# Start of a convolution and GRU kernel: loads on the software queue, taps in two parts, biases first

## The chip, the cores and the metric

The kernel runs on one core of a Trainium2 chip. Its time is the device time of one execution in microseconds. Three runs of the kernel before took 1042.65, 1043.94 and 1044.66 us; the median is 1043.94 us. One further execution was recorded with the hardware profiler; it took 1043.13 us, and the part that the profile shows, its span, is 1041.2 us. All times in this document that have the form of a place (such as "at 32.22") are us from the start of that span.

A core has a tensor engine (TensorE, in the profile PE for the products and PEld for the loads of the stationary operand), a vector engine (DVE), a scalar engine (ACT), GpSimd (POOL) and a sync engine (SP). SP, ACT and POOL can issue transfers from memory. SP and ACT issue on queues whose descriptors hardware makes (q1 and q10 in the profile); POOL issues on a software queue (q0).

## The reference

x is 16 sequences of 256 steps of 512 channels; cond is 16 x 512. The same cond serves twice: as the 16 taps of a causal depthwise convolution over time, and as the first hidden state of a GRU.

```python
    x = x + _L0_cond_ref(x, cond_2048[:, None, :])      # causal, 16 taps, one weight per tap and channel
    x = x + _L1_cond_ref(cond_2048, x, W_ih, W_hh, b_ih, b_hh)

        def cell(h, x):
            gi = x @ W_ih + b_ih
            gh = h @ W_hh + b_hh
            i_r, i_z, i_n = jnp.split(gi, 3, axis=-1)
            h_r, h_z, h_n = jnp.split(gh, 3, axis=-1)
            r = jax.nn.sigmoid(i_r + h_r)
            z = jax.nn.sigmoid(i_z + h_z)
            n = jnp.tanh(i_n + r * h_n)
            h_new = (1.0 - z) * n + z * h
            return (h_new, h_new)
```

All arithmetic is in float32. W_ih and W_hh are 512 x 1536, that is 3 MB each.

## The kernel before, in words

**Layout.** The 512 channels lie as four quarters q of 128 partitions (`NQ` = 4). Time is cut into 16 chunks of 16 steps (`CHUNKS`), a chunk's 16 steps x 16 sequences being 256 columns. For each chunk c: x is loaded into `x_nat` by eight transfers of 64 KB (`load_x`, two halves s of the steps times four quarters j); VectorE transposes it in two pieces into `xT` (`turn_units`), in front of which ScalarE copies the 15 earlier steps (`halo`); then the convolution is added up in `x1T`: a first term (x times 1 + the last tap, `first_terms`, ScalarE) and 15 taps a quarter (`tap_units`, VectorE, one instruction a tap and quarter, k = 0 of all four quarters first).

**Chunk 0** is different, since everything waits for it. Its quarters 0 and 1 are made on VectorE, with the taps of short reach first (`needed` = 14 instructions reach into the chunk's first eight steps), and its quarters 2 and 3 (`Q_PE`) on TensorE (`conv_on_tensor`): ScalarE scales an identity matrix by each tap's weights into 32 diagonal matrices `diag`, and TensorE multiplies x by them, tap after tap into one accumulator a quarter. Tap k reaches back `K - 1 - k` steps and writes the columns from `lag(k)` = 16 (15 - k) on; so columns 0 to 127 (the first eight steps) are done after the taps k = 15 to 8.

**Products.** `ni_units` makes the candidate's input products for a block of eight steps (`NI`), quarter by quarter, with W_ih's third part `wih_n`; ScalarE evicts each quarter and adds the bias `bnT` (`evict`). `pair_units` adds the input products of r and z for two steps into the accumulators `prz`, on top of the biases that `seed_rz` and `seed_nh` copied there from `b_rows`. `b_rows` comes from `spread_biases`: four products spread the bias rows `b_two` over the partitions into the accumulator `spare`, and ScalarE copies them out.

**Step** t (`step`): TensorE multiplies h by W_hh's parts R, N and Z (`recurrent`, L420), then does products of the next pair and of the next block (`other_products`); ScalarE takes r; VectorE, after its share of taps (`bulk_work`), multiplies r by N's product (`rn`, L446), transposes, adds, and ends with three scans (L472) whose result is the next h. The first `rn` on VectorE stands behind all taps that the program put in front.

**What sets the order.** The program's order is written by hand: each engine and queue works off its instructions in the order in which they are written. VectorE's taps and transpositions for the chunks 1 to 15 are units in a `Plan` with a cost and a step by which they are due; `bulk.run(0, HEAD)` does units of `HEAD` us in front of step 0, and each step does as many as the rate towards the due times asks for, five taps at most unless one is due. First terms and evictions are handed out from two lists (`firsts`, `evictions`) at the places where the program says so.

**Loads in front.** The taps' weights cond go out on SP and ScalarE; x's chunk 0 half on SP and ScalarE, half on POOL (L144); chunk 1 half on SP, half on POOL (L157); then the biases (L158 to L164) and W_ih by four transfers a part (`load_weights`: quarters 0 and 1 on SP, 2 and 3 on POOL). W_hh's twelve transfers are written later, behind `seed_nh` (L576): quarter 0 on SP, 1 on ScalarE, 2 and 3 on POOL, with R's on POOL kept behind the last part of W_ih. Before any product TensorE runs 108 tiny ones (`idle_products(PAD)`) and a drain.

Of the kernel before, what the change touches and what calls it, by code (L numbers as in the profile page):

```python
# [24 lines left out]
F32 = mybir.dt.float32  # L25
# [5 lines left out]
P = 128  # L31
L = 32
GT = 8
R, Z, N = 0, 1, 2
CHUNKS = (16,) * 16
PAD = 108
HEAD = 11.0
SYNC = mybir.DependencyInfo(mybir.DependencyClass.Sync, mybir.DependencyReason.DATA)
Q_PE = (2, 3)
NI = 8  # L40
# [35 lines left out]
def conv_gru_kernel(  # L76
# [31 lines left out]
    ps = ctx.enter_context(tc.tile_pool(name="ps", bufs=1, space=PSUM))  # L108
    ps_ni = ctx.enter_context(tc.tile_pool(name="ps_ni", bufs=2, space=PSUM))
# [9 lines left out]
    def load_x(c, queues=((nc.sync,), (nc.sync,)), behind=None):  # L119

        n = CHUNKS[c]
        t = xin.tile([P, max(CHUNKS) // 2, P], F32, tag="x_nat", name=f"x_nat_{c}")
        for s in range(2):
            for j in range(NQ):
                made = queues[s][j % len(queues[s])].dma_start(  # L125
                    out=t[32 * j + B * s : 32 * j + B * s + B, 0 : n // 2],
                    in_=x[:, starts[c] + s : starts[c] + n : 2, j * P : (j + 1) * P],
                )
                if s == j == 0 and behind is not None:
                    tc.add_manual_dep(made.ins, behind.ins.name, SYNC, reason="later in time")  # L130
        x_nat[c] = t
# [8 lines left out]
    for j in range(NQ):  # L140
        (nc.sync, nc.scalar)[j % 2].dma_start(
            out=cond_nat[32 * j : 32 * j + B, :], in_=cond[:, j * P : (j + 1) * P]
        )
    load_x(0, ((nc.sync, nc.scalar), (nc.gpsimd,)))  # L144
    nc.scalar.activation(warm, warm, AF.Sigmoid)
    ident = const.tile([P, P], F32)
    make_identity(nc, ident)
# [6 lines left out]
    bn_nat = const.tile([P, P], F32)  # L154
    nc.vector.memset(bn_nat, 0.0)

    load_x(1, ((nc.sync,), (nc.gpsimd,)))  # L157
    nc.sync.dma_start(out=b_two[0:1, :], in_=b_hh.rearrange("(o c) -> o c", o=1))  # L158
    nc.sync.dma_start(
        out=b_two[1:2, 0 : 2 * C], in_=b_ih[0 : 2 * C].rearrange("(o c) -> o c", o=1)  # L160
    )
    nc.gpsimd.dma_start(
        out=bn_nat[0:P:L, :], in_=b_ih[2 * C : 3 * C].rearrange("(j c) -> j c", j=NQ)
    )  # L164

# [1 line left out]
    wih_rz = const.tile([P, NQ, 2 * C], F32)  # L167
    wih_n = const.tile([P, NQ, C], F32)
    whh = [const.tile([P, NQ, C], F32, name=f"whh_{g}") for g in range(3)]

    def load_weights(w_sb, w, g, queues):
        return [
            queues[j].dma_start(
                out=w_sb[L * j : L * j + L],
                in_=w[j * P : (j + 1) * P, g * C : g * C + w_sb.shape[2]].rearrange(
                    "(q l) c -> l q c", l=L
                ),
            )
            for j in (0, 2, 1, 3)
        ]  # L180


    for tile_of, g in ((wih_n, N), (wih_rz, R)):
        of_wih = load_weights(tile_of, w_ih, g, (nc.sync, nc.sync, nc.gpsimd, nc.gpsimd))
    zero_z = [const.tile([P, NQ * B * 2], F32, name=f"zero_z_{i}") for i in range(2)]
    for t in zero_z:
        nc.gpsimd.memset(t, 0.0)
# [11 lines left out]
    b_rows = const.tile([P, 3, P], F32)  # L199


    xT, x1T, ni = {}, {}, {}
# [3 lines left out]
    evictions = []  # L206
# [7 lines left out]
    def turn_units(c):  # L214

        def halo():
            xT[c] = xtp.tile([P, NQ, HALO + CMAX], F32, tag="xT", name=f"xT_{c}")
            if c:
                m = CHUNKS[c - 1] * B
                nc.scalar.copy(xT[c][:, :, 0:HALO], xT[c - 1][:, :, m : m + HALO])  # L220

        def turn(a):
            o = HALO + a * PAIR
            nc.vector.transpose(  # L224
                xT[c][:, :, o : o + GT * B].rearrange("p q (a r) -> p a q r", r=L),
                x_nat[c][:, a : a + GP].rearrange("p a (q l) -> p a q l", q=NQ),
            )
            if 2 * (a + GP) == CHUNKS[c] and 4 < c + 3 < NCH:
                load_x(c + 3)

        return [(0.0, halo)] + [
            (0.7, lambda a=a: turn(a)) for a in range(0, CHUNKS[c] // 2, GP)
        ]

    def first_terms(c):

        x1T[c] = x1p.tile([P, NQ, CMAX], F32, tag="x1T", name=f"x1T_{c}")
        n = CHUNKS[c] * B

        def first(q):  # L240
            nc.scalar.activation(  # L241
                x1T[c][:, q, 0:n],
                xT[c][:, q, HALO : HALO + n],
                AF.Copy,
                scale=last1[:, q : q + 1],
            )
# [33 lines left out]
    def conv_on_tensor():  # L280

        n = CHUNKS[0] * B
        diag = const.tile([P, len(Q_PE), K, P], F32)

        def weight(k, q):
            return condT[:, q, k : k + 1] if k < K - 1 else last1[:, q : q + 1]

        for i, q in enumerate(Q_PE):
            for k in reversed(range(K)):
                nc.scalar.activation(diag[:, i, k], ident, AF.Copy, scale=weight(k, q))  # L290
        for i, q in enumerate(Q_PE):
            acc = ps_ni.tile([P, CHUNKS[0] * B], F32, tag="pni", name=f"conv_{q}")
            for k in reversed(range(K)):
                nc.tensor.matmul(  # L294
                    acc[:, lag(k) : n],
                    lhsT=diag[:, i, k],
                    rhs=xT[0][:, q, HALO : k * B + n],
                    start=(k == K - 1),
                    stop=(k == 0),
                    skip_group_check=True,  # L300
                )
            evictions.append(lambda q=q, acc=acc: nc.scalar.copy(x1T[0][:, q, 0:n], acc[:, 0:n]))


    blocks = [(t0, NI) for t0 in range(0, T, NI)]
# [39 lines left out]
    rz = [ps.tile([P, 2, P], F32, name=f"prz_{i}") for i in range(2)]  # L345
    nh = [ps.tile([P, P], F32, name=f"pnh_{i}") for i in range(2)]
    spare = ps.tile([P, 3, P], F32, name="spare")

    def mark():

        for i in range(2):
            nc.tensor.matmul(rz[i], lhsT=blank[:, 0:P], rhs=blank, start=True, stop=True)
            nc.tensor.matmul(nh[i], lhsT=blank[:, 0:P], rhs=blank[:, 0:P], start=True, stop=True)

    def idle_products(n):

        for _ in range(n):
            nc.tensor.matmul(
                spare[0:L, 0, 0:1], lhsT=blank[:, 0:L], rhs=blank[:, 0:1], start=True, stop=True
            )  # L360

    def spread_biases():
        for j in range(NQ):
            nc.tensor.matmul(
                spare[L * j : L * j + L],
                lhsT=ones,
                rhs=b_two.rearrange("o (g j c) -> o j g c", g=3, j=NQ)[:, j],
                start=True,
                stop=True,
            )  # L370
# [166 lines left out]
    bulk = Plan()  # L537
    mark()
    idle_products(PAD)
    nc.tensor.drain()  # L540
    (_, halo), *turns = turn_units(0)
    halo()
    for t in hist:
# [6 lines left out]
    for q in range(NQ):  # L550
        if q not in Q_PE:
# [2 lines left out]
                xT[0][:, q, HALO : HALO + CHUNKS[0] * B],  # L554
                last1[:, q : q + 1],
            )
    conv_on_tensor()

    taps = [fn for i, (_, fn) in reversed(list(enumerate(tap_units(0)))) if i % NQ not in Q_PE]
    needed = (NI - 1) * (NQ - len(Q_PE))  # L560
# [5 lines left out]
    for fn in taps[needed:]:  # L566
        fn()
    evictions.pop(0)()
    first_terms(1)
    give_firsts()  # L570
    evictions.pop(0)()
    spread_biases()
    nc.scalar.copy(b_rows, spare)
    seed_rz(0)
    seed_nh(0)
    for g in (R, N, Z):  # L576

        made = load_weights(whh[g], w_hh, g, (nc.sync, nc.scalar, nc.gpsimd, nc.gpsimd))
        if g == R:
            tc.add_manual_dep(made[2].ins, of_wih[0].ins.name, SYNC, reason="behind W_ih in time")  # L580
    for fn in ni_units(*blocks[0]):
        while evictions:
            evictions.pop(0)()
        fn()
    while evictions:
        evictions.pop(0)()
    for fn in pair_units(0):
        fn()
    for c in range(1, NCH):
        due = starts[c] - NI  # L590
        taps = tap_units(c)

        ahead = []
        if c + 1 < NCH:
            ahead = turn_units(c + 1) + [(0.0, lambda c=c: first_terms(c + 1))]
        at = len(taps) - AHEAD
        for cost, fn in taps[:at] + (ahead if c > 1 else []) + taps[at:]:
# [9 lines left out]
    for t in range(T):  # L607
        p, s = divmod(t, 2)
# [65 lines left out]
```

## Time and profile before

| what | value |
|---|---|
| median of three runs | 1043.94 us |
| the profiled execution, its own time | 1043.13 us |
| its span | 1041.2 us |
| TensorE products busy | 1023.8 us (98%) |
| VectorE busy | 926.6 us (89%) |
| ScalarE busy | 380.2 us (37%) |
| the chain that ended last | 96% TensorE, 1% VectorE, 1% transfers |
| first transposition of x | 7.64 |
| first product of step 0 | 32.22 |
| first `rn` of step 0 | 35.72 |
| first product of step 1 | 37.60 |

The lines of the profile are read like this. A line of the timeline or of the chain has its start and its length in us, the engine (with a q where only its sequencer or queue works), the line of the program, the operation, what it writes and reads by the program's names, the shape and a count; in square brackets stands how long the engine was idle before it and what ended that. A line of the stretches has for each engine its busy us and in brackets the number of instructions, then the clock that TensorE was granted (1.00 is full), the share of the 16 transfer engines' time, and GB/s. A line of the transfers has the size of one and the median us from issue to landing. A group by form has busy us and the mean ns of one instruction behind the bar.

### The profile page before, as it was taken

How to read it: one execution, taken by the hardware profiler on the slowest of the kernel's cores; microseconds unless marked ns; L12 is line 12 of the kernel's file. 1: busy time of each engine (PE TensorE's matmuls, PEld its weight loads, DVE VectorE, ACT ScalarE, POOL GpSimd, SP SyncE). 2: the span in 40 equal slices, each digit the busy share in tenths (PEclk: the TensorE clock that was granted, in tenths of full speed). 3: DMA queues.
4: the chain of work that ended last, by engine and by line, in shares of the span. 5: the costliest groups of instructions: out<-in, count | busy, mean ns of one | idle time of the engine just before them, and what ended most of it. 6: DMA issues, size and time to landing. Idle time of an engine off the chain costs nothing.

```text
span 1041.2 us, 71853 instructions
## 1 busy us (share of the span) xinstructions
PE 1023.8 (98%) x32952; PEld 929.9 (89%) x32952; DVE 926.6 (89%) x3606; ACT 380.2 (37%) x1520; POOL 11.4 (1%) x27
## 2 busy tenths in 40 slices
PE   7899999999999999999999999999999999999997
PEld 7789999999999999999999999999999999999986
DVE  7899999999999999999999999999999999996555
ACT  6243433434333343433334333343333334333332
POOL 4000000000000000000000000000000000000000
PEclk9999999999999999999999999999999999999999
DMA  9320100101010010100100010010000000000000
GB/s 232 93 60 8 32 14 20 30 15 27 13 34 15 15 34 6 34 14 15 35 15 25 15 33 16 14 33 7 14 15 14 14 13 5 15 15 14 14 11 17
DMA packets 40978, 27.72 MB, mean 27 GB/s; under 512 B 6686, under 2 KB 38498, under 8 KB 40676
## 3 DMA queue, kind: packets, MB, share of 16 engines
q1 hardware_dynamic: 38612, 18.52, 7.9%
q8 instruction: 257, 4.21, 1.8%
q0 software_dynamic: 1216, 3.67, 1.3%
q10 hardware_dynamic: 848, 0.95, 0.4%
q14 instruction: 45, 0.37, 0.1%
HBM read 14.73 MB, written 8.39 MB: 22 GB/s over the span
## 4 chain that ended last, share of the span: by engine, by line
PE 96%; DVE 1%; DMA 1%; ACT 0%; issue 0%; POOL 0%; SPq 0%; DVEq 0%; POOLq 0%
PE prz L420 42%; PE pnh L420 21%; PE prz L385 20%; PE pni L322 10%; PE conv L294 1%; DMA whh<-in_L_cond_W_hh_dram 1%; DMA x_nat<-in_x_dram 0%; DVE rnT L448 0%; DVE rn L446 0%; DVE zp L459 0%; DVE n L450 0%; DVE xT L224 0%; ACT zero_z L463 0%; POOL x_nat L125 0%; DVE hist L472 0%
## 5 line engine op out<-in xcount | busy, mean ns | idle before, releaser
L420 PE MATMUL prz<-whh,hist 128*32 128x128 f32 x16320 | 539.4, 273 | 2.2 <-DVE hist L472 1.3
L420 PEld LDWEIGHTS prz<-whh,hist 128*32 128x32 f32 x16320 | 449.7, 104 | 7.3 <-DVE hist L472 5.3
L267 DVE SCALAR_TENSOR_TENSOR x1T<-xT,condT,x1T 128x256 f32<-128x256 f32 (+2 forms) x930 | 377.3, 462 | 0.6 <-ACT x1T L241 0.6
L420 PE MATMUL pnh<-whh,hist 128*32 128x128 f32 x8160 | 269.6, 273 | 0.0
L385 PE MATMUL prz<-wih_rz,x1T 128*32 128x256 f32 x4096 | 268.0, 379 | 0.0
L420 PEld LDWEIGHTS pnh<-whh,hist 128*32 128x32 f32 x8160 | 226.5, 104 | 0.0
L457 ACT ACTIVATE dn<-n 128x64 f32<-128x64 f32 x256 | 67.9, 265 | 325.1 <-DVE n L450 325.1
L385 PEld LDWEIGHTS prz<-wih_rz,x1T 128*32 128x32 f32 x4096 | 128.4, 110 | 43.8
L322 PEld LDWEIGHTS pni<-x1T,wih_n 128*32 128x32 f32 x4096 | 122.4, 110 | 43.7 <-ACT ni L334 0.8
L437 ACT ACTIVATE r<-prz 128x128 f32<-128x128 f32 x256 | 70.9, 277 | 240.5 <-PE prz L420 237.7
L322 PE MATMUL pni<-x1T,wih_n 128*32 128x128 f32 x4096 | 157.9, 273 | 0.6 <-ACT ni L334 0.6
L472 DVE TENSOR_TENSOR_SCAN hist<-zero_z,dn 128x32 f32<-128x32 f32 (+1 forms) x768 | 128.5, 216 | 0.0
L446 DVE TENSOR_TENSOR rn<-r,pnh 128x128 f32<-128x128 f32 x256 | 72.3, 282 | 38.7 <-PE pnh L420 37.4
L463 ACT ACTIVATE zero_z<-zp 128x32 f32<-128x32 f32 x512 | 90.8, 226 | 6.9
L448 DVE STREAM_TRANSPOSE rnT<-rn 128x128 f32<-128x128 f32 x256 | 79.7, 311 | 8.8
L459 DVE STREAM_TRANSPOSE zp<-prz 128x128 f32<-128x128 f32 x256 | 80.8, 316 | 0.1
L334 ACT ACTIVATE ni<-pni,bnT 128x128 f32<-128x128 f32 x128 | 46.9, 367 | 75.7 <-PE pni L322 75.7
L465 DVE TENSOR_TENSOR dn<-hist,dn 128x64 f32<-128x64 f32 x255 | 58.3, 229 | 11.4
L450 DVE TENSOR_TENSOR n<-rnT,ni 128x64 f32<-128x64 f32 x256 | 57.6, 225 | 8.9
L400 DVE COPY glance<-r 1x1 f32<-1x1 f32 x256 | 34.1, 133 | 28.3 <-ACT r L437 28.2
L373 ACT COPY prz<-b_rows 128x256 f32<-128x256 f32 x128 | 48.6, 379 | 0.0
L400 DVE COPY glance<-zero_z 1x1 f32<-1x1 f32 x256 | 36.4, 142 | 7.9
(51 smaller groups left out, 214.6 us busy)
## 6 DMA issues: line engine op xcount, KB each, us to landing
out_dram<-o SPq DMA_DIRECT2D x248, 32.0 KB, 1.7
x_nat<-in_x_dram SPq DMA_DIRECT2D x118, 64.0 KB, 3.0
whh<-in_L_cond_W_hh_dram POOLq DMA_DIRECT2D x6, 256.0 KB, 14.2
wih_rz<-in_L_cond_W_ih_dram POOLq DMA_DIRECT2D x2, 512.0 KB, 10.9
wih_rz<-in_L_cond_W_ih_dram SPq DMA_DIRECT2D x2, 512.0 KB, 12.7
whh<-in_L_cond_W_hh_dram SPq DMA_DIRECT2D x3, 256.0 KB, 15.4
whh<-in_L_cond_W_hh_dram ACTq DMA_DIRECT2D x3, 256.0 KB, 9.8
x_nat<-in_x_dram POOLq DMA_DIRECT2D x8, 64.0 KB, 4.9
```

The costliest lines, as they stand in the source:

```text
L267: nc.vector.scalar_tensor_tensor(out=x1T[c][:, q, to], in0=xT[c][:, q, k * B + to.start : k * B + n], scalar=condT[:, q, k : k + 1], in1=x ...
L322: nc.tensor.matmul(hold[q][32 * j : 32 * j + 32, 0:n], lhsT=wih_n[:, kc, j * P + q * L : j * P + q * L + L], rhs=x1T[c][:, kc, o : o + n], ...
L385: nc.tensor.matmul(rz[p % 2][32 * j : 32 * j + 32], lhsT=x1T[c][:, kc, o : o + PAIR], rhs=w_rz[:, :, j * P : (j + 1) * P], start=False, st ...
L400: nc.vector.tensor_copy(glances[i][0:1], of_scalar[0:1, 0:1])
L420: product = nc.tensor.matmul(dst[32 * j : 32 * j + m], lhsT=h[0](kc), rhs=whh[g][:, kc, j * P : (j + 1) * P], start=False, stop=(kc == NQ ...
L437: of_r = nc.scalar.activation(r, pr, AF.Sigmoid)
L446: nc.vector.tensor_mul(rn, r, pnh)
L448: nc.vector.transpose(rnT, by_part(rn))
L457: nc.scalar.activation(dn_v[:, :, :, 1], n, AF.Tanh)
L459: nc.vector.transpose(zp, by_part(pz))
L463: nc.scalar.activation(z_v[:, qs, :, 1], zp[:, qs, half], AF.Sigmoid) for qs in halves
L472: nc.vector.tensor_tensor_scan(hist_g[:, lo + at : lo + end], z[:, to], dn[:, to], 0.0, op0=ALU.mult, op1=ALU.add,)
```

## The change

- x's chunks 0 and 1 are loaded by POOL alone, 16 transfers. The bias row `bn_nat` goes to SP.
- All of W_hh is issued together with W_ih: SP has quarter 0 of all parts and quarter 1 of W_ih and of R; POOL has the rest; ScalarE issues none. The dependency that held R back is gone. POOL's two clears of `zero_z` now stand behind all its transfers.
- `spread_biases` and the copy into `b_rows` stand first on TensorE and ScalarE, in front of the diagonals; a second drain stands in front of them.
- `conv_on_tensor` makes its taps in two parts. The taps k = 15 to 8 of both quarters come first, and ScalarE evicts the first eight steps' columns; the taps k = 7 to 0 come behind the candidate's first block and in front of the first input products of r and z. The accumulators are now a tile of their own and `spare`.
- Chunk 1's first terms come one by one behind the evictions of the candidate's first block. Before, all four came before that block.
- `HEAD` is 9.3 instead of 11.0, which makes 23 taps instead of 27 in front of step 0. Chunk 2's transpositions and first terms are due with chunk 1's taps, in front of the last ten of them; before they were due four steps later.

```diff
-HEAD = 11.0
+HEAD = 9.3
...
-    load_x(0, ((nc.sync, nc.scalar), (nc.gpsimd,)))
+    load_x(0, ((nc.gpsimd,), (nc.gpsimd,)))
...
-    load_x(1, ((nc.sync,), (nc.gpsimd,)))
+    load_x(1, ((nc.gpsimd,), (nc.gpsimd,)))
...
-    nc.gpsimd.dma_start(
+    nc.sync.dma_start(
         out=bn_nat[0:P:L, :], in_=b_ih[2 * C : 3 * C].rearrange("(j c) -> j c", j=NQ)
     )
...
-    for tile_of, g in ((wih_n, N), (wih_rz, R)):
-        of_wih = load_weights(tile_of, w_ih, g, (nc.sync, nc.sync, nc.gpsimd, nc.gpsimd))
+    for tile_of, w, g in (
+        (wih_n, w_ih, N),
+        (wih_rz, w_ih, R),
+        (whh[R], w_hh, R),
+        (whh[N], w_hh, N),
+        (whh[Z], w_hh, Z),
+    ):
+        second = nc.gpsimd if tile_of is whh[N] or tile_of is whh[Z] else nc.sync
+        load_weights(tile_of, w, g, (nc.sync, second, nc.gpsimd, nc.gpsimd))
...
-        for i, q in enumerate(Q_PE):
-            acc = ps_ni.tile([P, CHUNKS[0] * B], F32, tag="pni", name=f"conv_{q}")
-            for k in reversed(range(K)):
...
-            evictions.append(lambda q=q, acc=acc: nc.scalar.copy(x1T[0][:, q, 0:n], acc[:, 0:n]))
+        def taps(ks, to):
+            for i, q in enumerate(Q_PE):
+                for k in ks:
+                    nc.tensor.matmul(
+                        conv[i][:, lag(k) : n],
+                        lhsT=diag[:, i, k],
+                        rhs=xT[0][:, q, HALO : k * B + n],
+                        start=(k == K - 1),
+                        stop=(k == 0),
+                        skip_group_check=True,
+                    )
+                evictions.append(
+                    lambda i=i, q=q: nc.scalar.copy(x1T[0][:, q, to], conv[i][:, to])
+                )
+
+        return [
+            lambda: taps(range(K - 1, K - 1 - NI, -1), slice(0, NI * B)),
+            lambda: taps(range(K - 1 - NI, -1, -1), slice(NI * B, n)),
+        ]
...
+    conv = [
+        ps.tile([P, CHUNKS[0] * B], F32, name="conv_0"),
+        spare.rearrange("p g c -> p (g c)")[:, 0 : CHUNKS[0] * B],
+    ]
...
     nc.tensor.drain()
+    nc.tensor.drain()
...
-    conv_on_tensor()
+    spread_biases()
+    nc.scalar.copy(b_rows, spare)
+    needed_first, needed_later = conv_on_tensor()
+    needed_first()
...
     evictions.pop(0)()
-    first_terms(1)
-    give_firsts()
     evictions.pop(0)()
-    spread_biases()
-    nc.scalar.copy(b_rows, spare)
     seed_rz(0)
     seed_nh(0)
-    for g in (R, N, Z):
-
-        made = load_weights(whh[g], w_hh, g, (nc.sync, nc.scalar, nc.gpsimd, nc.gpsimd))
-        if g == R:
-            tc.add_manual_dep(made[2].ins, of_wih[0].ins.name, SYNC, reason="behind W_ih in time")
+    first_terms(1)
     for fn in ni_units(*blocks[0]):
         while evictions:
             evictions.pop(0)()
+            give_firsts(1)
         fn()
+    while evictions:
+        evictions.pop(0)()
+    give_firsts()
+    needed_later()
...
-        for cost, fn in taps[:at] + (ahead if c > 1 else []) + taps[at:]:
+        for cost, fn in taps[:at] + ahead + taps[at:]:
             bulk.add(cost, due, fn)
-        if c == 1:
-            for cost, fn in ahead:
-                bulk.add(cost, due + GT // 2, fn)
```

More of the change, by code (lines that the diff above doesn't have):

```diff
@@ L171, in load_weights @@
     def load_weights(w_sb, w, g, queues):
-        return [
+        for j in (0, 2, 1, 3):
             queues[j].dma_start(
@@ L178, in load_weights @@
             )
-            for j in (0, 2, 1, 3)
-        ]
-    for tile_of, g in ((wih_n, N), (wih_rz, R)):
-        of_wih = load_weights(tile_of, w_ih, g, (nc.sync, nc.sync, nc.gpsimd, nc.gpsimd))
+    for tile_of, w, g in (
[7 more added lines that the diff above has]
+        load_weights(tile_of, w, g, (nc.sync, second, nc.gpsimd, nc.gpsimd))
     zero_z = [const.tile([P, NQ * B * 2], F32, name=f"zero_z_{i}") for i in range(2)]
@@ L290, in conv_on_tensor @@
                 nc.scalar.activation(diag[:, i, k], ident, AF.Copy, scale=weight(k, q))
-        for i, q in enumerate(Q_PE):
-            acc = ps_ni.tile([P, CHUNKS[0] * B], F32, tag="pni", name=f"conv_{q}")
-            for k in reversed(range(K)):
[L294 to L300, printed above, removed]
-                )
-            evictions.append(lambda q=q, acc=acc: nc.scalar.copy(x1T[0][:, q, 0:n], acc[:, 0:n]))
+        def taps(ks, to):
[11 more added lines that the diff above has]
+                    lambda i=i, q=q: nc.scalar.copy(x1T[0][:, q, to], conv[i][:, to])
+                )
+        return [
+            lambda: taps(range(K - 1, K - 1 - NI, -1), slice(0, NI * B)),
+            lambda: taps(range(K - 1 - NI, -1, -1), slice(NI * B, n)),
+        ]
     blocks = [(t0, NI) for t0 in range(0, T, NI)]
```

## The prediction

> **What bounds the kernel now.** I read the page first (engines, slices), then the chain of waits over the first 60 us, then the timeline, the stretches and the forms of single instructions there. TensorE is busy 98% of the span, and past the first steps each step takes 3.92 us (rn starts at 91.16 and 95.08), an order of products that the change leaves alone. So the change is worth what it does before step 0's end and in the dozen steps behind it. The chain of waits there:
>
> ```profile
> 2.98 4.39 DMA x_nat<-in_x_dram
> ...
> 7.64 1.32 DVE xT L224 x2
> ...
> 9.09 11.82 PE conv L294 x64
> 20.91 0.82 PE spare L364 x8
> ...
> 21.76 0.49 ACT b_rows L573
> ...
> 22.33 9.64 DMA whh<-in_L_cond_W_hh_dram
> 31.97 0.25 issue
> 32.22 2.00 PE prz L420 x29
> ```
>
> Read it downwards: x lands, its transposition, all 32 taps of the convolution, the biases, and only then, from ScalarE's queue behind its copies, the last quarter of W_hh, which lands 9.6 us later. Then the stretches (busy us of PE, PEld, DVE, ACT, POOL; granted clock; DMA share; GB/s):
>
> ```profile
> 26.00:28.00 2.00, 1.82 (x36) 0.82 (x28) 2.00 (x6) 0.37 (x1) 0.00 (x0) 1.00 1.05 309
> 28.00:30.00 2.00, 0.00 (x0) 0.00 (x0) 2.00 (x7) 0.00 (x0) 0.00 (x0) 1.00 1.06 247
> 30.00:32.00 2.00, 0.00 (x0) 0.00 (x0) 1.65 (x5) 0.00 (x0) 0.00 (x0) 0.91 0.67 131
> 32.00:34.00 2.00, 1.78 (x31) 1.60 (x35) 0.00 (x0) 0.00 (x0) 0.00 (x0) 0.50 0.07 20
> ```
>
> TensorE idles over 4 us, and its first step then runs at a granted clock of 0.50. The DMA engines are full until 30 us: bytes bound this part almost as much as the late issue. VectorE is busy nearly as long, with taps put ahead of step 0:
>
> ```profile
> 29.59 2.05 DVE L267 SCALAR_TENSOR_TENSOR x1T<-xT,condT,x1T 128x256 f32<-128x256 f32 x5
> ...
> 34.84 0.14 DVE L400 COPY glance<-r 1x1 f32<-1x1 f32 x1 [3.20 <-ACT r L437]
> 35.72 0.29 DVE L446 TENSOR_TENSOR rn<-r,pnh 128x128 f32<-128x128 f32 x1 [0.73 <-PE pnh L420]
> ```
>
> Its taps end at 31.64 and step 0's rn starts at 35.72: at most 4 us can be had before VectorE itself is the bound. This rn is my yardstick; the next step's first product follows 1.88 us later (37.60).
>
> **The loads.** x goes through GpSimd's queue alone. Four issues there take 2.21 us from 1.30, so the eighth of chunk 0 starts near 5.06; now the fourth, at 2.98, is the last to land. What lands how soon:
>
> ```profile
> x_nat<-in_x_dram POOLq DMA_DIRECT2D x1, 64.0 KB, 2.8
> x_nat<-in_x_dram POOLq DMA_DIRECT2D x2, 64.0 KB, 5.6
> ```
>
> The first row is the queue's first issue, with little else in flight, the second those at 5.1 to 5.6 us, behind x loads of three queues. SP and ScalarE issue no x any more, and SP's weights can start near 4 us, so I take 3.3, nearer the light row: landing at 8.4, the transposition at 8.6 in place of 7.64, with bounds of 7.9 and 10.7 for the landing. Chunk 1's last issue moves from 5.60 to 9.8 and lands by 13.1 to 15.6; VectorE wants it at 15.2, so this is free or costs 0.4. The identity matrix, now behind eight x loads instead of four, is ready at 6.2 instead of 4.1; the biases below come later. bn_nat moves to SP, where it precedes the weights: one issue, hidden, since its transposition comes after 16 us.
>
> W_ih for the candidate: GpSimd's half is issued at 10.3 to 11.4 instead of 6.7 to 7.8, behind eight more x loads; it took 7.1 us (6.7 to 7.4), so 17.4 to 18.8. SP's half starts earlier. W_hh: SP now issues its part by 7 us, without waits behind W_ih as now (up to 3.2 us each), and ScalarE issues none. In bytes, nothing is less: 7.3 MB. GpSimd's queue carries 4.5 MB of them in the order x, W_ih, R, N, Z. At the measured 300 GB/s the whole ends near 30 us; R lands near 25, N near 27.5, Z near 30.
>
> One rule speaks against the move. The Trainium skill ("SBUF — State Buffer", the trap of VectorE blocking software DMAs) says that GpSimd cannot write descriptors while VectorE runs an operation in a two-port mode. In this trace GpSimd's x and weight issues keep 0.53 to 0.58 us, from 1.9 us on, also beside VectorE's transpositions and taps. By the rule at most the two scalings at 9 us (0.35 each) would hold chunk 1 back, by 0.7; the sum stays as it is.
>
> **Biases first.** b_hh and b_ih are issued at 2.8 and 3.1 (VectorE clears b_two until 2.75) instead of 5.1 and 5.5, and land near 5.3, as cond's rows do after 1.7 to 2.1 us; with the 5.3 us of the crowded bn_nat it would be 8.4. The four products took 0.85; TensorE is at half rate then, so 1.6. The copy into b_rows (0.48) now stands in front of ScalarE's 32 diagonals, which start at 7.4 instead of 4.41. Diagonals and halo copy take 10.33 us (4.41 to 14.75), so ScalarE is free at 17.75. That is the price of this part: 3 us on ScalarE, now slack (it waits 1.7 us at 14.75 and 2.5 at 18.4), then no longer.
>
> **The taps split.** The same form at 9 us and at 16 us, from the groups by form of two stretches:
>
> ```profile
> L294 PE MATMUL conv<-xT,diag 128*128 128x256 f32 x2 | 1.2, 700 | 4.1 <-DVE xT L224 4.1
> L294 PE MATMUL conv<-xT,diag 128*128 128x256 f32 x2 | 0.7, 420 | 0.0
> ```
>
> The first eight taps of quarter 2 ran slowly, 9.09 to 14.56 (5.47 us); quarter 3's eight took 2.79, and the later eight of a quarter 1.7. From the transposition to the first tap is 1.45 us now, so conv starts near 10.0, and the sixteen early taps are through near 18.4 with the clock coming up about as long after the start as now. (If it comes up a window of 3.4 us earlier or later, about 0.8 earlier, held by ScalarE's 17.75, or 1.0 later.) The sixteen later taps, 3.4 us, go behind the block.
>
> On this the Trainium skill ("TensorE: Matmul & The Clock Gate", What's actually happening) says that the activity window is free-running, so the moment of full rate moves from run to run. No single trace shows that; it would make of my 18.4 anything from 17.75 to 19.4.
>
> ScalarE then copies both halves (until 18.7), seeds rz and nh (0.31 and 0.26, until 19.2) and works in turn: eviction of ni, first term of chunk 1. The block is 0.875 us a quarter (21.62 to 23.37 for two). So TensorE's block runs as if from 18.05 and ends at 21.55, and the fourth first term ends at 22.6: it stands behind the fourth eviction, where now all four are done at 18.4. VectorE's taps of chunk 1 start with k = 0 of each quarter and so wait for it. VectorE arrives at 18.89 + 0.9 = 19.8 and waits about 1.6 us in all. From 22.65 it has 25 taps left: 28 (23 of HEAD, five of step 0) less three, where now it has 32. At 0.398 (12.75 us for 32) that is 9.95: rn at 32.65 instead of 35.72, **3.07 us earlier**. The removed cover matters: each us that the block slips comes back whole.
>
> TensorE meanwhile: later taps to 24.95, input products (1.73) to 26.7, R at once (W_hh there since 25), N and Z as they land, Z done by 31.2; rn's chain wants Z at 33.4. No idle of 4 us is left before R, so that half-rate stretch goes too; it is in the 3.07.
>
> **The steps behind.** The four taps taken out of HEAD come back, and chunk 2's transpositions, four steps earlier in due time, stand among chunk 1's. In the changed program steps 1 to 4 have five taps, steps 5 and 6 one transposition each with two and three taps, step 7 seven taps; now it is five, five, then four. Five taps give 3.93 to 3.98 us a step, nearly free. Seven: VectorE's 1.90 besides taps (75.57 to 77.47) plus 7 x 0.407 is 4.75, so +0.83. Against that a stall goes:
>
> ```profile
> 67.20 0.48 DVE L267 SCALAR_TENSOR_TENSOR x1T<-xT,condT,x1T 128x256 f32<-128x256 f32 x1 [0.58 <-ACT x1T L241]
> 67.60 0.13 DVE L400 COPY glance<-r 1x1 f32<-1x1 f32 x1
> 67.66 0.27 DVE L446 TENSOR_TENSOR rn<-r,pnh 128x128 f32<-128x128 f32 x1
> ```
>
> This step lasts 4.45 (from rn at 63.21), 0.53 too long, since the first term comes just after its transposition; with the transposition two steps ahead it is there in time. The five-tap steps add 0.1: **+0.4** in all, between -0.3 (all absorbed) and +1.2 (stall kept, or moved). From step 13 on VectorE's order is the same in both programs.
>
> **Sum:** -3.07 + 0.4 = -2.7 us. The profiled execution took 1043.13 (its span 1041.2), giving 1040.4; it lay 0.8 under the median 1043.94 of runs from 1042.65 to 1044.66. I take half of that as the part of the spread that stays: **1040.8**.
>
> **Rivals.** *Covered anyway:* the candidate's W_ih lands at 20 to 21 rather than 18, or the biases at 6.5 to 8. Then the block and with it the fourth first term slip by 1 to 3 us, and of the 2.7 between 1.7 and nothing is left: 1041.8 to 1043.9. For it speaks that the engines are full at 200 GB/s while x moves; against, that x in 512 B pieces is no longer spread over three queues. *Slower:* GpSimd's queue is starved beside SP's large packets. In the stretch 3 to 9 us it moved 0.45 MB, 75 GB/s. At that rate 1 MB of x ends near 17 instead of 13.1 and W_ih near 24: the block starts at 24 instead of 18.05, rn at 38.6, 2.9 late, with the 0.4 of the steps and the 0.4 of the offset 1046.8. It decides from a landing of W_ih past 20.9. Against it, from 20 to 26 us the same queue moved 1.13 MB beside SP's 0.64. *The change doesn't do what it says:* W_hh is bound by bytes and Z comes at 33, as now. VectorE's slack of 2 us covers it; cost 0 to 0.5, so 1041.3. It is inside the forecast.
>
> **How the numbers follow.** Forecast (1039.2 to 1041.8, the last rival within): 0.58. Covered: 0.27. Slower by over 0.2%: 0.15. 0.2%, 2.1 us, is about what this measurement can tell from no change. The low end, 1039.2, is VectorE without any wait for first terms (19.8 + 28 x 0.398 = 30.95, 1.7 more, nearly all of it); the high end, 1045.2, takes in the covered case and the lighter starved ones.
>
> **What would show it.** Right: no W_hh wait before R; first rn near 32.6 right after taps; VectorE waiting for first terms between 19 and 23; a step of 4.7 us at step 7 and none of 4.45 after it. Wrong: a wait of the block for wih_n, conv starting after 11 us, slow taps past 17 us.

## The result, and the profile after

The changed kernel took 1052.14 us in the median of four runs (1050.29 to 1052.71), against 1043.88 us for the kernel before in four runs beside it (1042.65 to 1044.66): a ratio of 1.0074, 95% interval 1.0059 to 1.0088. It is slower by 8.3 us, where 2.7 us less than the profiled execution of before was forecast. The profiled execution took 1052.71 us with a span of 1050.8 us, so 9.6 us more span than before.

Nearly all of it arises before the end of step 0. The first `rn` starts at 44.98 instead of 35.72 (+9.3 us); from there to the `rn` of step 13 the changed kernel takes 51.67 us and the kernel before 51.52. The chain of waits of the changed kernel, over the first 60 us (start, length, what):

```profile
5.09 8.42 DMA x_nat<-in_x_dram
13.51 0.28 issue
13.79 9.65 DMA x_nat<-in_x_dram
23.57 1.30 DVE xT L229 x2
...
25.07 3.10 DVE x1T L272 x15
28.22 5.97 PE pni L335 x128
...
35.02 9.99 DVE x1T L272 x25
45.05 0.21 DVE rn L464
```

Before, x held this chain for 4.39 us and W_hh for 9.64. Now it is x for 18 us: an eighth load of chunk 0 that needs 8.42 us to land, and a load of chunk 1 that needs 9.65. The timeline of TensorE, VectorE and GpSimd says what waited (start, length, engine, line, in brackets the idle time before and what ended it):

```profile
15.09 4.97 PE L299 MATMUL conv<-xT,diag 128*128 128x256 f32 x16 [7.60 <-ACT diag L295]
28.22 5.93 PE L335 MATMUL pni<-x1T,wih_n 128*32 128x128 f32 x128 [5.46 <-DVE x1T L272]
43.16 1.07 PE L438 MATMUL prz<-whh,condT 128*16 128x128 f32 x32 [1.72 <-DMA whh<-in_L_cond_W_hh_dram]
```

```profile
13.63 1.30 DVE L229 STREAM_TRANSPOSE xT<-x_nat 128x512 f32<-128x512 f32 x2 [9.49 <-DMA x_nat<-in_x_dram]
15.63 4.70 DVE L272 SCALAR_TENSOR_TENSOR x1T<-xT,condT,x1T 128x240 f32<-128x240 f32 x14
23.57 1.30 DVE L229 STREAM_TRANSPOSE xT<-x_nat 128x512 f32<-128x512 f32 x2 [3.25 <-DMA x_nat<-in_x_dram]
31.01 0.48 DVE L272 SCALAR_TENSOR_TENSOR x1T<-xT,condT,x1T 128x256 f32<-128x256 f32 x1 [2.70 <-ACT x1T L246]
35.02 9.99 DVE L272 SCALAR_TENSOR_TENSOR x1T<-xT,condT,x1T 128x256 f32<-128x256 f32 x25 [0.39 <-ACT x1T L246]
```

```profile
13.79 0.53 POOL L125 DMA_DIRECT2D x_nat<-in_x_dram  x1 [1.84 <-DMA x_nat<-in_x_dram]
15.72 0.57 POOL L173 DMA_DIRECT2D wih_n<-in_L_cond_W_ih_dram  x1 [1.40 <-DMA x_nat<-in_x_dram]
16.55 0.55 POOL L173 DMA_DIRECT2D wih_n<-in_L_cond_W_ih_dram  x1 [0.26 <-DMA x_nat<-in_x_dram]
...
28.31 0.55 POOL L173 DMA_DIRECT2D whh<-in_L_cond_W_hh_dram  x1 [1.29 <-DMA wih_n<-in_L_cond_W_ih_dram]
```

The transposition of chunk 0 comes 6 us late, chunk 1's 9.3 us late. The profile puts the block's wait down to VectorE's taps, but the 14 taps that the block needs had ended at 20.33 (the later taps are no condition: with the pieces cut, below, the block starts at 20.25, in the middle of them); what came at 28.2 is the last GpSimd quarter of the candidate's W_ih, for which a GpSimd issue also waits until 28.31. GpSimd could issue that quarter only at 16.55, because its own issues now wait for earlier x loads to land. The block itself took 5.97 us (3.7 in later runs at full clock), since the granted clock was 0.5 from 26.03 to 32.85. The transfers of the changed kernel from 8 to 23 us, by queue (packets, MB, share of the 16 engines), and its stretches (busy us of PE, PEld, DVE, ACT, POOL; granted clock; DMA share; GB/s):

```profile
q1 hardware_dynamic: 860, 2.09, 80.5%
q0 software_dynamic: 322, 0.66, 24.9%
```

```profile
15.00:20.00 5.00, 4.91 (x17) 4.55 (x18) 4.96 (x16) 3.25 (x10) 2.31 (x5) 1.00 1.03 168
25.00:30.00 5.00, 1.78 (x36) 1.81 (x40) 3.31 (x17) 0.00 (x0) 1.10 (x2) 0.60 1.05 203
```

SP's weights, which nothing needs yet, moved 2.09 MB (139 GB/s) while GpSimd's queue, with x and the first weights behind it, moved 0.66 MB (44 GB/s). The transfer engines were full in the two stretches, yet moved 168 and 203 GB/s, where before it was 313 and 277.

### The profile page after: what moved, and what is told of

Same layout as the page of the kernel before. It is cut to its first block, busy times and chain, and to the rows that moved or that the text cites. A ratio compares the mean times of both kernels' runs of the same rounds, so it can differ in the third digit from the quotient of the medians.

```text
span 1050.8 us, 71856 instructions
## 1 busy us (share of the span) xinstructions
PE 1025.2 (98%) x32952; PEld 929.4 (88%) x32952; DVE 926.5 (88%) x3606; ACT 380.6 (36%) x1522; POOL 16.2 (2%) x36
## 4 chain that ended last, share of the span: by engine, by line
PE 94%; DVE 3%; DMA 2%; POOL 0%; ACT 0%; issue 0%; SPq 0%; DVEq 0%; POOLq 0%
PE prz L438 42%; PE pnh L438 21%; PE prz L403 20%; PE pni L335 11%; DMA x_nat<-in_x_dram 2%; DVE x1T L272 2%; POOL x_nat L125 0%; DVE rnT L466 0%; DVE rn L464 0%; DVE zp L477 0%; DVE n L468 0%; ACT zero_z L481 0%; DVE hist L490 0%; DVE glance L418 0%; DMA out_dram<-o 0%
## 5 line engine op out<-in xcount | busy, mean ns | idle before, releaser
L418 DVE COPY glance<-r 1x1 f32<-1x1 f32 x256 | 34.0, 133 | 25.3 <-ACT r L455 25.3
```

What stands on the lines that cost most here:

```text
L418: nc.vector.tensor_copy(glances[i][0:1], of_scalar[0:1, 0:1])
```

## The experiments

Three theories for the loss. **A, turns:** the transfer engines take one piece from each queue in turn, so a queue's share of the bytes goes as the size of its pieces, and x in runs of 512 B starves beside weights in runs of 2 and 4 KB. **B, software queue:** GpSimd's queue is slow in itself. **C, order:** the new order of biases, taps and first terms costs by itself.

**x alone put back.** The changed kernel with x on its queues of before:

```diff
-    load_x(0, ((nc.gpsimd,), (nc.gpsimd,)))
+    load_x(0, ((nc.sync, nc.scalar), (nc.gpsimd,)))
...
-    load_x(1, ((nc.gpsimd,), (nc.gpsimd,)))
+    load_x(1, ((nc.sync,), (nc.gpsimd,)))
```

> The changed kernel, with x loaded on the queues of the kernel before (chunk 0 half on SP and ScalarE, half on GpSimd; chunk 1 half on SP, half on GpSimd); all else as changed. Theory A (turns: the DMA engines serve the queues piece by piece, x's pieces are 512 B and the weights' 2 to 4 KB, so x starves on a queue beside another queue's weights): with x ahead of SP's weights on SP's own queue the first transposition starts by 8.5, the candidate's W_ih lands by 19, the first rn starts at 32 to 34.5; 1040 to 1043.5 us. Theory B (GpSimd's software queue is slow in itself or served last, whatever it carries): half of x is still on it, chunk 0 lands by 8.5 as before since only four loads are on it, time 1041 to 1046. Theory C (the new order of biases, taps and first terms costs the time, the loads do not): first rn past 40, 1048 us or more.

1046.33 us (1044.94 to 1048.55) beside 1044.28 for the kernel before, ratio 1.0017 (1.0008 to 1.0027). Each against the kernel before beside it, 2.0 of the 8.3 us are left, and the gain that A expected is not there. The timeline of TensorE shows what was missed:

```profile
11.07 1.50 PE L382 MATMUL spare<-b_two,ones 2*32 2x384 f32 x8 [6.07 <-DVE xT L229]
13.46 4.92 PE L299 MATMUL conv<-xT,diag 128*128 128x256 f32 x16 [0.89 <-ACT diag L295]
...
22.29 0.64 PE L335 MATMUL pni<-x1T,wih_n 128*32 128x128 f32 x16 [1.17 <-DMA wih_n<-in_L_cond_W_ih_dram]
```

The bias rows now stand behind x on SP and are spread only at 11.07 (5.98 in the changed kernel; the products read nothing of the transposition that the profile names), and ScalarE's diagonals, behind them, start at 13.01. So "biases first" has a price that x decides.

**x alone moved.** The kernel before with only x on GpSimd:

```diff
-    load_x(0, ((nc.sync, nc.scalar), (nc.gpsimd,)))
+    load_x(0, ((nc.gpsimd,), (nc.gpsimd,)))
...
-    load_x(1, ((nc.sync,), (nc.gpsimd,)))
+    load_x(1, ((nc.gpsimd,), (nc.gpsimd,)))
```

> The kernel before, with only its x loads of chunks 0 and 1 moved to GpSimd's queue; biases, taps, W_hh, HEAD as before. Theories A and B: the first transposition starts at 11 to 14 instead of 7.64, chunk 1 lands past 18, step 0's first rn starts at 40 to 46 instead of 35.72; 1048 to 1055 us. Theory C: first transposition by 9, first rn by 37.5, 1046 us at most.

One run: 1053.31 us, first transpositions at 15.00 (A and B had 11 to 14) and 24.80, first `rn` at 45.13. This one edit makes the whole loss, with the order of before. C falls as its cause.

**SP's weights held behind x.** In the changed kernel, SP's first weight load waits for the last load of chunk 1:

```diff
...
+            if w_sb is wih_n and j == 0:
+                tc.add_manual_dep(made.ins, of_x.ins.name, SYNC, reason="behind x in time")
```

> The changed kernel, with SP's first load of weights waiting until chunk 1's last x load on GpSimd's queue has landed; nothing else is moved. Theory A: x alone on its queue, with nothing beside it: chunk 0 landed by 8.5, chunk 1 by 14, the candidate's W_ih by 18, the last of W_hh near 34 (6.3 MB from 13 us on at 300 GB/s); first rn at 33 to 35.5; 1041.5 to 1045 us. Theory B: chunk 0 still lands past 11 and chunk 1 past 19, with SP's weights only behind it; first rn past 45, more than 1052 us. Theory C: chunk 1 by 14, but first rn past 40, 1048 us or more.

x lands as A says: chunk 0's transposition at 8.64, and chunk 1 landed by 13.06, when SP's first weight load goes out; all of it is still on GpSimd, so the software queue is not slow in itself. The time is 1053.75 us all the same (ratio 1.0092, 1.0077 to 1.0107), and A's time is missed. TensorE's timeline, and the transfers from 13 to 19 us, say why:

```profile
27.56 5.59 PE L338 MATMUL pni<-x1T,wih_n 128*32 128x128 f32 x128 [9.68 <-DMA wih_n<-in_L_cond_W_ih_dram]
```

```profile
DMA packets 345, 1.22 MB, mean 203 GB/s; under 512 B 47, under 2 KB 47, under 8 KB 345
q0 software_dynamic: 345, 1.22, 105.4%
```

SP's part of W_ih was issued at 13.06, but for six us its queue moved nothing: GpSimd's weights ran alone, at 203 GB/s. The wait moved from x to the weights. That SP's queue got no turn at all for six us is not what A says.

**The queues swapped.** x and GpSimd's share of the weights on SP, SP's share on GpSimd, biases on ScalarE:

```diff
-    load_x(0, ((nc.gpsimd,), (nc.gpsimd,)))
+    load_x(0, ((nc.sync,), (nc.sync,)))
...
-        second = nc.gpsimd if tile_of is whh[N] or tile_of is whh[Z] else nc.sync
-        load_weights(tile_of, w, g, (nc.sync, second, nc.gpsimd, nc.gpsimd))
+        second = nc.sync if tile_of is whh[N] or tile_of is whh[Z] else nc.gpsimd
+        load_weights(tile_of, w, g, (nc.gpsimd, second, nc.sync, nc.sync))
```

> The changed kernel with the two queues' loads exchanged: all of x and what was GpSimd's share of the weights on SP, SP's share of the weights on GpSimd, the three bias loads on ScalarE. Theory A: now x starves on the hardware queue beside GpSimd's weights: chunk 0 lands at 11 to 16, chunk 1 past 19, 1049 us or more. Theory B: x on the hardware queue lands at 8 to 9 (chunk 0) and 13 to 15 (chunk 1), 1040 to 1045 us. Theory C: as B for the loads, but 1048 us or more.

One run: 1056.37 us, transpositions at 22.40 and 29.01. Now x starves on a hardware queue. Its transfers from 9 to 17 us:

```profile
q0 software_dynamic: 427, 1.43, 88.2%
q1 hardware_dynamic: 455, 0.21, 16.0%
```

427 packets beside 455, 1.43 MB beside 0.21: nearly equal turns and unequal bytes, as A has it, though chunk 0 came even later than A's 11 to 16. B is refuted: x is late on either queue beside the other queue's weights.

A's count does not come out of the changed kernel itself, though. Its transfers from 8 to 13 us, while x is late:

```profile
DMA packets 336, 1.00 MB, mean 200 GB/s; under 512 B 78, under 2 KB 78, under 8 KB 336
q1 hardware_dynamic: 242, 0.81, 87.6%
q0 software_dynamic: 94, 0.19, 18.9%
```

No packet there lies between 512 B and 2 KB: x's runs of 512 B cross GpSimd's queue in packets of 4 KB, as large as those of the weights. And the turns are not equal: 94 packets beside 242, and 51 beside 252 from 5 to 8 us. So x on GpSimd's queue is late because it gets fewer turns, not because its packets are small; what gives it fewer is open.

**The pieces cut.** The changed kernel with SP's weight loads in pieces of 128 columns:

```diff
+            piece = P if queues[j] is nc.sync else wide
+            for a in range(0, wide, piece):
...
-                out=w_sb[L * j : L * j + L],
+                    out=w_sb[L * j : L * j + L, :, a : a + piece],
```

> The changed kernel with the weight loads of SP cut into pieces of 128 columns: 512 B runs instead of 2 and 4 KB, the same bytes on the same queue, 40 loads instead of 10. Turn theory (the DMA engines take one piece from each queue in turn, so bytes go by the size of a piece): x and SP's weights now move at equal rates, some 90 KB/us each of the 180 KB/us that both moved in the changed kernel; of chunk 0's 512 KB some 230 have landed by 5 us, so the first transposition comes at 8 to 9.5 us (13.63 in the changed kernel) and chunk 1's at 14 to 15.5 (23.57); the block's first product at 20 to 25 and the time 1041 to 1047. Rival 'shared bytes' (the queues share the bandwidth by bytes or by who came first, and the size of a piece is nothing): 13 to 14 and 23 to 24, time 1050 to 1054.

One run: transpositions at 10.22 and 17.07, 3.4 and 6.5 us earlier than in the changed kernel with the same bytes on the same queues, though 0.7 and 1.6 us past A's range. So the size of SP's pieces bears on x: from 6 to 15 us the two queues moved about equal bytes (0.72 MB on GpSimd's, 0.68 on SP's), in unequal packets (336 and 1509). (40 issues also spread SP's load over more time; but its queue moved 47 to 105 KB in each us from 6 to 14, less than the 128 that 64 KB every half us allow.) The time, 1052.52 us, is no better than the changed kernel's, since SP's own weights in small pieces now come late: first W_ih's part for r and z, for which TensorE waits until 36.44, then W_hh. The transfers from 20 to 33 us:

```profile
q0 software_dynamic: 775, 2.60, 88.2%
q1 hardware_dynamic: 830, 0.38, 16.4%
```

Here, with weights on both queues, the turns are nearly equal; SP's quarters of W_hh, in small pieces too, ran alone from 35 to 43 us at 112 to 144 KB in each us, and step 0's first product with W_hh came at 39.98.

**Biases off SP.** The first experiment, with `b_two` on ScalarE's queue behind chunk 0 and `bn_nat` on GpSimd:

```diff
+    nc.scalar.dma_start(out=b_two[0:1, :], in_=b_hh.rearrange("(o c) -> o c", o=1))
+    nc.scalar.dma_start(
+        out=b_two[1:2, 0 : 2 * C], in_=b_ih[0 : 2 * C].rearrange("(o c) -> o c", o=1)
+    )
...
-    nc.sync.dma_start(out=b_two[0:1, :], in_=b_hh.rearrange("(o c) -> o c", o=1))
...
-    nc.sync.dma_start(
+    nc.gpsimd.dma_start(
         out=bn_nat[0:P:L, :], in_=b_ih[2 * C : 3 * C].rearrange("(j c) -> j c", j=NQ)
```

> The first experiment (the changed kernel with x on the queues that it had before) with b_two's two loads on ScalarE's queue right behind its part of chunk 0, and bn_nat's load on GpSimd as before the change; so no bias stands behind x on SP. Theory 'the biases only came late': b_two lands at 6 to 8 us, diagonals from 7 to 8.5, the first tap on TensorE 8.5 to 10 (13.46 in the first experiment), SP's quarters of W_ih earlier too, first step's rn at 36 to 38.5 (39.32), time 1042.5 to 1045.5. Rival 'the order costs by itself' (diagonals behind the biases, taps cut in two, the block in front of the long taps): the diagonals come early and the time stays at 1046 to 1048.

1044.98 us beside 1045.26, ratio 0.9999 (0.9988 to 1.0010). The time is in the theory's favour; the diagonals, at 10.81, and the first tap on TensorE, at 11.27, are not as early as expected, since `b_two` landed at 8.85. The block starts at 18.84, but its later quarters wait until 21.36 for ScalarE, which copies out TensorE's taps only behind the diagonals. The first `rn` comes at 35.47, behind VectorE's taps, and TensorE waits for Z's weights until 35.01.

**Weights balanced.** The same, with the second quarter of W_hh's N and Z on SP:

```diff
-        second = nc.gpsimd if tile_of is whh[N] or tile_of is whh[Z] else nc.sync
+        second = nc.sync
```

> The kernel of the run before with one more line changed: the second quarter of W_hh's N and Z goes to SP instead of GpSimd, so the two queues carry about the same bytes. Theory (one queue alone moves about 195 KB/us, two together about 300): both queues end at 29 to 33 us instead of GpSimd's alone at 36 to 43; step 0 no longer waits for W_hh's Z; first rn 35 to 37.5, time 1039.5 to 1044, and under 1043.9 it beats both kernels. Rival (the order of taps and first terms holds step 0 back, not the weights): within 0.5 us of the run before.

1044.42 us, ratio 0.9998 (0.9989 to 1.0008). By the numbers it is the rival: 0.6 us from the run before, and no change that can be told. Its reason holds in part: the block ran at half the clock from 21.9 to 25.3, the last first term ended at 26.98 and VectorE's taps held the first `rn` until 36.98. But balancing did not bring W_hh forward either: TensorE waits for Z until 35.34.

**W_hh early, alone.** The kernel before, W_hh issued behind W_ih on SP and GpSimd:

```diff
+    for g in (R, N, Z):
+        load_weights(whh[g], w_hh, g, (nc.sync, nc.sync, nc.gpsimd, nc.gpsimd))
...
-    for g in (R, N, Z):
-        made = load_weights(whh[g], w_hh, g, (nc.sync, nc.scalar, nc.gpsimd, nc.gpsimd))
...
```

> The kernel before with W_hh alone moved: issued right behind W_ih, two quarters of each gate on SP and two on GpSimd, none on ScalarE and no wait; x, biases, taps and first terms as before. Theory 'x on the other queue is the only loss': no loss here: x's two transpositions at 7.6 and 14.2 us as before, the first rn at 34.5 to 36, time 1042 to 1044.5. Rival 'weights issued early push out what is needed first': W_ih or x lands over 1 us later than before, first rn past 37, time over 1045.

1043.86 us beside 1045.26, ratio 0.9991 (0.9982 to 1.0000): the best of all, and not told from no change. Its chain of waits:

```profile
10.78 20.83 DMA whh<-in_L_cond_W_hh_dram
31.61 0.14 issue
31.75 1.91 PE pnh L422 x32
33.65 1.71 PE prz L422 x32
35.36 1.71 PE prz L387 x16
37.07 0.68 PE pni L324 x16
37.74 0.87 PE prz L422 x32
```

The first `rn` is 2.0 us earlier than before (33.71), but N's last part lands at 31.6 even so, and the next four groups run at half the clock (0.5 from 30.60 to 37.42, before from 31.62 to 35.03; N's 32 products take 1.91 us, later 0.87). Step 0 to 1 takes 5.84 us instead of 4.07, and by step 13 0.13 us of the 2.0 is left.

**TensorE kept busy in the waits.** That kernel with 90 one-column products in step 0:

```diff
+        if t == 0:
+            idle_products(20)
         recurrent(pr, R)
+        if t == 0:
+            idle_products(70)
```

> The run with W_hh alone moved early, plus products of one column on TensorE in the waits of step 0: 20 in front of R's products and 70 behind them (108 of them took 3.79 us at the start, so 0.7 and 2.5 us), to fill the idle time from 26.6 to 31.7 us before W_hh's N lands. Theory 'the clock falls to a half because TensorE stood idle in a window of 3.41 us': no stretch at 0.5 between 27 and 40 us, N's and Z's products of step 0 take 0.9 us each instead of 1.9 and 1.7, step 0 to 1 takes 4.0 to 4.2 us instead of 5.84, the time 1041 to 1042.8 against about 1045 for the kernel before on this chip (ratio 0.996 to 0.9985), which beats both kernels. Rival 'products of one column do not count, or the half clock comes from something else': stretch and step stay, and the time is within 0.5 us of 1043.9.

1046.00 us beside 1043.62, ratio 1.0020 (1.0011 to 1.0029). The clock is still 0.5 from 32.16 to 38.98, and two idle times appear behind the small products that the profile can't explain ("1.85 <-issue", "1.34 <-issue"). The rival's sign holds, its size not: the products cost. Since the waits were not filled throughout, why the clock fell stays open.

**The order with everything early.** The balanced kernel with `b_two` in front of x (a row each on SP and ScalarE) and the same 90 products:

```diff
+    nc.vector.memset(b_two[:, 2 * C : 3 * C], 0.0)
+    nc.sync.dma_start(out=b_two[0:1, :], in_=b_hh.rearrange("(o c) -> o c", o=1))
+    nc.scalar.dma_start(
+        out=b_two[1:2, 0 : 2 * C], in_=b_ih[0 : 2 * C].rearrange("(o c) -> o c", o=1)
+    )
     load_x(0, ((nc.sync, nc.scalar), (nc.gpsimd,)))
```

> The changed kernel's order of diagonals, taps, block and first terms, with everything that came late for it mended: x and bn_nat on their queues of before, b_two's two rows in front of x (one on SP, one on ScalarE), W_hh two quarters each on SP and GpSimd, the same one-column products in the waits of step 0. Theory 'the order was sound and worth little, since W_hh's bytes set the end of step 0 in any order': diagonals from 5.5 to 7.5 us, first tap on TensorE 8.5 to 9.5, the block from 16 to 18.5, W_hh's last part at 31.5 to 34, first rn 33 to 35.5, and a time within 1 us of the run that it shares the chip with. Rival 'the order is worth the 3 us of the prediction': first rn 32.7 or earlier and over 1 us faster than that run. Rival 'the order itself costs': over 1 us slower.

1046.32 us, ratio 1.0027 (1.0015 to 1.0039), within 0.3 us of the run beside it. Diagonals at 7.20, taps at 9.27, the block at 17.85, W_hh's N at 33.50: as the theory had them; the first `rn`, 37.04, is later, with 1.24 us of idle in N's products as above. So the same without the small products:

```diff
-        if t == 0:
-            idle_products(20)
         recurrent(pr, R)
-        if t == 0:
-            idle_products(70)
```

> The run before (the changed kernel's order with x, biases and W_hh early) without the 90 one-column products in step 0. Theory 'the products cost, the order does not': the idle stretch behind them that the profile calls issue (1.24 us) goes, N's products of step 0 run in one piece, first rn 34 to 36 (37.04), time 1.5 to 3 us less than that run, 1042.5 to 1045 on a chip where the kernel before takes 1043.6 to 1045.3. Rival 'the order itself costs': first rn 36.5 or later, and over 1 us slower than the kernel before. Rival 'the order is worth 3 us': over 1.5 us faster than the kernel before.

1044.86 us beside 1043.34, ratio 1.0013 (1.0004 to 1.0022), first `rn` at 36.77. By its numbers that is the rival "the order itself costs", and by 1.5 us. The timelines of VectorE and of TensorE name another cause:

```profile
23.20 9.98 DVE L272 SCALAR_TENSOR_TENSOR x1T<-xT,condT,x1T 128x256 f32<-128x256 f32 x25 [0.39 <-ACT x1T L246]
33.10 0.13 DVE L418 COPY glance<-r 1x1 f32<-1x1 f32 x1
36.77 0.29 DVE L464 TENSOR_TENSOR rn<-r,pnh 128x128 f32<-128x128 f32 x1 [3.53 <-PE pnh L438]
```

```profile
29.80 1.07 PE L438 MATMUL prz<-whh,condT 128*16 128x128 f32 x32 [1.92 <-DMA whh<-in_L_cond_W_hh_dram]
34.80 1.91 PE L438 MATMUL pnh<-whh,condT 128*16 128x128 f32 x32 [3.94 <-DMA whh<-in_L_cond_W_hh_dram]
```

VectorE was ready at 33.2 and waited 3.5 us for N, and TensorE 3.9 us for N's weights. These came 3 us later than with W_hh early alone. In part the loads started worse: x's first transposition is at 9.50 (7.66 there), with SP's x issues held until `b_two` had landed (the chain has "5.13 0.31 SPq L125" behind that landing). But that differs from one execution to the next: the run before has the same loads in the same order and x's transposition at 7.82, and N's weights came at 33.50 all the same. So neither the place of the biases nor the order is shown to cost here, and why N's weights come later than with W_hh early alone stays open.

## Why the prediction was wrong, step by step

- **The loads: this step failed.** "I take 3.3, nearer the light row" and a landing of W_ih at 17.4 to 18.8 became 8.42 us for chunk 0 (13.5 instead of 8.4), 23.4 for chunk 1 (by 13.1 to 15.6) and 28.2 for W_ih. Both rows that I bounded it with were taken mostly beside other x loads: the first had no weights on the other queue beside it, the second only its last 3 us, and the upper end, 10.7, was no bound. Freeing SP early, counted as an advantage, is what starved x: with SP's weights held back, x is transposed at 8.64, as predicted (8.6).
- **The row that was read wrongly.** Against the starved rival I set "1.13 MB beside SP's 0.64" in the stretch 20 to 26 us. The full rows of before:

```profile
q0 software_dynamic: 347, 1.13, 64.4%
q1 hardware_dynamic: 345, 0.64, 38.9%
```

  Here GpSimd's queue carried weights, in packets of 4 KB, and got 347 turns beside 345. With x on it, in packets of 4 KB too, it got 94 beside 242. A row with other loads on the queue was no evidence against the rival.
- **The starved rival** had the place and the order of events right, and was given 0.15 and a price that was too low: 75 GB/s from a stretch beside x, where 44 were measured beside weights. It gave W_ih at 24 and `rn` at 38.6; measured 28.2 and 44.98. W_ih was also issued 5 us later than written (15.7 and 16.6, not 10.3 to 11.4), since GpSimd's issues wait for earlier x loads. The rest is the half clock in the block: 5.97 us for 3.5.
- **"Each us that the block slips comes back whole": right.** Last first term at 34.98 instead of 22.6, then 25 taps in 9.99 us (9.95 predicted): `rn` 12.3 us past the predicted 32.65.
- **W_hh "bound by bytes": too small.** R near 25, N near 27.5, Z near 30 took 300 GB/s from the start. The kernel before moved 190 GB/s from 5 to 10 us, while x was in flight, and 249 from 10 to 15. With W_hh early and nothing else moved, R's products started at 27.30, N's at 31.75 and Z's at 33.40. So the wait that was to go is mostly still there: with x on its queues of before, step 0's products wait for some part of W_hh until 31.8 to 35.6 us, and no run came to the predicted 32.65. The best, 33.71, was also held by N's products at half the clock. So even with x in time the forecast gain was not there. The third rival, W_hh bound by bytes, named this, but its price of 0 to 0.5 us was too low.
- **Biases, taps, block: right in size.** `b_rows` done at 8.0 and diagonals at 7.92 (7.4), transposition to first tap 1.46 us (1.45), the sixteen early taps 7.7 us (8.4). With x and biases early the block started at 17.85 and 18.64 (18.05) and the last first term ended at 22.39 and 23.17 (22.6).
- **The steps behind: right.** +0.15 us to step 13 (+0.4, from -0.3 to +1.2). The stall of 0.53 is gone (that step took 4.45, the two with a transposition now take 3.77 and 3.92), and the seven-tap step takes 4.82 (4.75), as VectorE's timeline of the changed kernel has it from one `rn` to the next:

```profile
68.49 0.29 DVE L464 TENSOR_TENSOR rn<-r,pnh 128x128 f32<-128x128 f32 x1
...
70.48 2.83 DVE L272 SCALAR_TENSOR_TENSOR x1T<-xT,condT,x1T 128x256 f32<-128x256 f32 x7
...
73.31 0.27 DVE L464 TENSOR_TENSOR rn<-r,pnh 128x128 f32<-128x128 f32 x1
```

- **The two rules that were cited.** The Trainium skill ("SBUF — State Buffer", the trap of VectorE blocking software DMAs) was rightly given no share: VectorE stood idle from 4.1 to 13.6 while x starved. What it says ("TensorE: Matmul & The Clock Gate", What's actually happening) of a free-running window agrees with these runs: in four of them TensorE's first tap starts between 9.09 and 9.27 us, and the full clock is granted at 13.53, 14.55, 15.09 and 15.37; the half-clock stretches inside the span last 3.4 us or a multiple. The half clock alone moved the block's end by 2.2 us in the changed kernel (5.93 us of products, 3.70 at full clock), most of the forecast gain.

## What to carry to other kernels

A load that is needed first can be starved by another queue's weights, on a software queue and on a hardware queue: x got 0.19 MB beside 0.81 on GpSimd's queue and 0.21 beside 1.43 on SP's. Turns of equal count explain the second pair and not the first, so read packets and bytes of each queue in the stretch in question, and do not carry a row over from a stretch with other loads. Smaller pieces on the other queue helped x (3.4 and 6.5 us) and hurt the weights; holding the weights back helped x and made W_ih late. An early issue of weights is no free gain while a load that is needed first is in flight. Before shortening the work ahead of a step, work out when the bytes that the step needs can have landed, at the rates of each stretch and not at the best one.

## What had not been expected of the hardware

- One queue alone moved 203 GB/s (SP's weights held back, 13 to 19 us) and 209 (the changed kernel, 24 to 40 us, GpSimd's queue); two queues of weights together 296 in the kernel before (20 to 26 us), but 196 with SP's weights held back (31 to 33 us). So a second queue does not always bring the higher rate, and no run here shows what does.
- A queue that starts behind a busy one may get nothing for some us: SP's from 13 to 19 us with its weights held back, and nearly nothing (0.01 MB beside 0.91) from 9 to 14 us in the first experiment. No run here shows the cause.
- An issue can stand on its queue until an earlier transfer has landed: 0.3 to 2.4 us at a time on GpSimd in the changed kernel.
- One-column products in TensorE's waits left idle times of 1.85 and 1.34 us, did not keep the clock, and cost 0.2%.
